# Four-layer graph network on one core: the first weights of layer 2 made inside layer 1, and every weight made one batch ahead of its product

## The chip, the cores and the metric

One core of one Trainium2 chip runs the whole program. The metric is device microseconds (us) of one execution; lower is better. Three runs of the kernel before gave 1958.09, 1960.70 and 1961.96 us, so the median is 1960.7 us.

The core has five engines that run side by side, each through its own fixed list of instructions: TensorE (PE; its weight loads are shown as PEld), VectorE (DVE), ScalarE (ACT), GpSimd (POOL) and SyncE (SP, which issues the transfers). An instruction starts when the one ahead of it on its engine is through and when the semaphores that it waits for are set. So an instruction that waits holds up everything behind it on its engine.

## The reference

There are 16 batches of 1024 nodes with 64 features, and one adjacency matrix for all. Each layer attends over neighbours, adds the result to `x` and normalises; the layers follow each other.

```python
x = _layernorm(x + _L0_gnn_ref(x, L0_gnn_W, L0_gnn_a, adj), axis=-1)
x = _layernorm(x + _L1_gnn_ref(x, L1_gnn_w0, L1_gnn_b0, L1_gnn_wa, L1_gnn_ba, adj), axis=-1)
x = _layernorm(x + _L2_gnn_ref(x, adj, L2_gnn_W, L2_gnn_a), axis=-1)
x = _layernorm(x + _L3_gnn_ref(x, adj, L3_gnn_Wh, ...), axis=-1)

def _L2_gnn_ref(input, adj, W, a):
    h = jnp.matmul(input, W)
    s1 = jnp.einsum('bnf,f->bn', h, a[:Fout, 0])
    s2 = jnp.einsum('bnf,f->bn', h, a[Fout:, 0])
    e = s1[:, :, None] + s2[:, None, :]
    e = jnp.where(e > 0, e, ALPHA * e)
    masked = jnp.where(adj[None, :, :] > 0, e, NEG_INF)
    attention = jax.nn.softmax(masked, axis=-1)
    return jax.nn.elu(jnp.matmul(attention, h))
```

## The kernel before, in words

The program is `fast_path`; a general path behind it runs only when a check at the end asks for it. P is 128, D is 64, N is 1024, C = 8 chunks of 128 nodes, B = 16 batches. `x` stays in four tiles of SBUF, one for each group of four batches.

**Layer 2** is `gat_layer(..., zero_mean=True)`. For batch b and chunk k, `unit` (L1011) is one DVE instruction (L1013) over 128x1024 elements: the larger of `G` and a factor `q`, times the adjacency `aT`. It is the masked weight `e` of chunk k, without its division. `product` (L1019) feeds it to four PE passes (L1025), which add up the batch's sum `y` over its eight chunks. What surrounds them, for a pair of batches (b, b+1 with b even):

- `prep_x` (PE transposes, ACT copies), `prep_s` (PE) and `prep_top` (DVE, then a POOL all-reduce) find the scores and their maximum.
- `prep_p`: DVE computes `down` and `up` (L958, L960), ACT computes `p` and `q` (L963, L965).
- `prep_G(b, h)` for the halves h = 0, 1: two matmuls into a PSUM tile `pg` (L978), which has one buffer in layer 2, and one ACT exponential (L987) into `G`. So the matmuls of half 1 wait for the exponential of half 0.
- `prep_v`: eight ACT scalings and a copy (L997, L999) into `vals`, the weights of the product.
- the ends of a batch: `evict` (ACT, L1044), `project` (PE, L1057), `divide` (DVE, L1100, L1102), `quotients` (eight ACT scalings L1112 and an exponential L1123), `residual` (DVE, L1128, L1129), `norm` (DVE, L1136 and, for odd b, seven small ones from L760 on), `root` and `shift` (ACT, DVE), `store` (eight ACT scalings, L780).

The order is written out by hand. `go` walks steps (t, k), t the batch and k the chunk: at each it makes `unit(k)` of batch t, lets the product of two units earlier follow (`LAG`), and then runs the tasks that the table `slots` has for (t, k). A place such as (-1, 4) in `places` means batch b's task stands at step (b-1, 4). The engines keep this order. `store` stands at (b+4, 0) for even b and at (b+3, 4) for odd b, so both fall in steps with t even; `prep_p`, `prep_G` of a pair stand at (b-1, 1), (b-1, 4) and (b-1, 6), in steps with t odd. The tile `e` has 7 buffers in layer 2.

**Layer 1** comes before it, in four groups of four batches. `product_l1` (L1898) adds up `po` for a chunk `ic` with 16 matmuls over the group's halves `hi` and `lo`; `average` (L1909) follows with two ACT instructions (L1912, L1913) and, on DVE, four of 128x256 (L1915, L1916, L1917, L1920) and four of statistics (L1922). `po` has two buffers in PSUM, and L1917 is the last reader of one. `hi` and `lo` have two buffers each. This layer is not in a hand-written order: the scheduler places its instructions and those that are put into its `ahead` lists. Eight of layer 2's first tasks (`l2_ahead[:8]`: `prep_x`, `prep_s`, `prep_top`, `prep_p` and the matmuls of `prep_G` for batches 0 and 1) go into the last group; the two exponentials into `G` and `prep_v(0)` come after it, at L2033, since their tiles are in a pool that opens there. The last group's own normalisation (`last`) is spread over layer 2's first steps: its statistics at (0, 0) and (0, 1), its ACT rows at (0, 3), (0, 7), (1, 3), (1, 7).

**Layer 3** follows. Its first preparations are placed in layer 2's steps (15, 0) to (15, 7). The ends of the last batches stand at (16, 0) to (16, 5), ahead of layer 3's first scores (PE, L1384), exponentials (ACT, L1388) and masks (DVE, L1392).

Of the kernel before, what the change touches and what calls it, by code (L numbers as in the profile page):

```python
# [8 lines left out]
F32 = mybir.dt.float32  # L9
F32R = mybir.dt.float32r  # L10
# [6 lines left out]
P = 128  # L17
# [20 lines left out]
LAG = 2  # L38
# [544 lines left out]
def fast_path(  # L583
# [25 lines left out]
    B, N, D = x.shape  # L609
# [301 lines left out]
    def gat_layer(w, name, zero_mean, own, room=None):  # L911
# [6 lines left out]
        xT, G, pgs, pq, vals, only, stats = {}, {}, {}, {}, {}, {}, {}  # L918
        if not zero_mean:
            ring = [gp.tile([P, C, 32], F32, tag=f"only{r}", name=f"only{r}", bufs=1) for r in range(4)]  # L920
            for t in ring:
# [56 lines left out]
                nc.tensor.matmul(parts[i], w1[rows, :], xT[b][h][rows, :], start=True, stop=True)  # L978

        def exps_G(b, h):  # L980
            if h == 0:
                G[b] = gp.tile([P, 2, N], F32, tag="G", name=f"G_{name}_{b}")
            cols = slice(h * HALF, (h + 1) * HALF)
            parts = pgs[b, h]
            for i, part in enumerate(parts):
                dst = G[b][:, :, cols] if len(parts) == 1 else G[b][:, i, cols]
                nc.scalar.activation(dst, part, AF.Exp, bias=pq[b][2], scale=1.0 - ALPHA)  # L987

        def prep_G(b, h):
            scores_G(b, h)  # L990
# [1 line left out]

        def prep_v(b):
            p = pq[b - b % 2][0][:, :, b % 2]
            v = gp.tile([P, C, D], F32, tag="vals", name=f"vals_{name}_{b}", bufs=3)
            for c in range(C):
                nc.scalar.activation(v[:, c, :F], xb(b)[:, c, :F], AF.Copy, scale=p[:, c : c + 1])  # L997
            if zero_mean:
                nc.scalar.copy(v[:, :, F], p)  # L999
            else:  # L1000
                only[b] = ring[b % 4]
                nc.scalar.copy(only[b][:, :, b % 2], p)
            vals[b] = v

        def attention(b):
# [3 lines left out]
            begins, closes = b % 2 == 0 or not joint, b % 2 == 1 or not joint  # L1009

            def unit(k):  # L1011
                e = gp.tile([P, N], F32, tag="e", name="e", bufs=7 if zero_mean else 10)
                nc.vector.scalar_tensor_tensor(  # L1013
                    e, G[b - b % 2][:, b % 2, :], pq[b - b % 2][1][:, k, b % 2 : b % 2 + 1], aT[:, k, :],
                    ALU.max, ALU.mult,
                )
                return e
# [164 lines left out]
        for b in range(0, B, 2):  # L1182
            halves = (range(CH), range(CH, C)) if zero_mean else (range(C), ())
            chain = [
                lambda b=b: prep_x(b, 0), lambda b=b: prep_x(b, 1), *(lambda b=b, c=c: prep_s(b, c) for c in halves),
                lambda b=b: prep_top(b), lambda b=b: prep_p(b), lambda b=b: prep_G(b, 0),
                lambda b=b: prep_G(b, 1), lambda b=b: prep_v(b), lambda b=b: prep_v(b + 1),
            ]
            if zero_mean:
                places = (-2, 0), (-2, 1), (-2, 5), (-2, 6), (-2, 7), (-1, 1), (-1, 4), (-1, 6), (-1, 2), (0, 4)  # L1190
            else:
                places = (-3, 3), (-3, 3), (-3, 7), (-3, 7), (-2, 1), (-2, 3), (-2, 7), (-1, 3), (-1, 4), (0, 4)
            if b == 0 and not zero_mean:
                chain[6:8] = [lambda f=f, h=h: f(0, h) for f in (scores_G, exps_G) for h in range(2)]
                ahead = chain[:-1]
                at(0, 4, chain[-1])
                continue
            if b == 2 and not zero_mean:
                places = (-2, 4), (-2, 5), (-2, 6), (-2, 6), (-2, 6), (-2, 7), (-1, 1), *places[7:]
            for task, (t, k) in zip(chain, places):  # L1200
                if b + t >= 0:
                    at(b + t, k, task)
                elif b:
                    at(0, 0, task)
                else:
# [555 lines left out]
    def prep_l1(g, q):  # L1761
# [36 lines left out]

        def back():
            if q == 0:  # L1800
                his[g] = l1["halves"].tile([P, C, 2, 2, P], F32R, tag="hi", name=f"hi{g}")
                los[g] = l1["halves"].tile([P, C, 2, 2, P], F32R, tag="lo", name=f"lo{g}")
            t = h["t"]
            pe = l1["psum"]("pe")
            for c in range(C):
                nc.tensor.transpose(pe[:, c, :], t[:, c, :], ident)
            hi, lo = his[g][:, :, q, 1, :], los[g][:, :, q, 1, :]
            nc.scalar.copy(hi, pe)
            nc.vector.tensor_tensor(h["f"], h["f"], pe, ALU.mult)
            nc.vector.tensor_tensor(lo, pe, hi.bitcast(F32), ALU.subtract)  # L1810
# [11 lines left out]
    with tc.tile_pool(name="ps_g", bufs=1, space=bass.MemoryType.PSUM, reuse_waits="tile") as ps_g, tc.tile_pool(  # L1822
# [64 lines left out]
    l2_ahead, l2_go = gat_layer(later["w2"], "l2", True, 6, room=dict(  # L1887
        xT=lambda: [ep.tile([P, C, D], F32, tag="v", name="xT").rearrange("p c d -> p (c d)") for _ in range(2)],
        g=lambda: l1["psum"]("pg").rearrange("p (i c) q -> p i (c q)", i=2),
    ))  # L1890
    l1_psum = ExitStack()
    ps_l = l1_psum.enter_context(tc.tile_pool(name="ps_l", bufs=2, space=bass.MemoryType.PSUM, reuse_waits="tile"))
    with tc.tile_pool(name="l1", bufs=2, reuse_waits="tile") as pool:
# [36 lines left out]
        for g in range(NG):  # L1930
            ahead = [[] for _ in range(C)]
            for q in range(2 if g + 1 < NG else 0):

                for ic, task in zip((q, q, q, q, q + 1, q + 2, q + 2, q + 4, q + 5), prep_l1(g + 1, q)):
                    ahead[ic].append(task)
            if g + 1 == NG:
                for ic, task in zip((1, 2, 3, 3, 4, 5, 6, 6), l2_ahead):
                    ahead[ic].append(task)
            st = pool.tile([P, C * GB, 6], F32, tag="st1", name=f"st{g}")
            for ic in range(C):  # L1940
                po = product_l1(g, ic)
# [15 lines left out]
    l1_pools.close()  # L1957

    l3a = ctx.enter_context(tc.tile_pool(name="l3a", bufs=2, side="right", reuse_waits="tile"))

# [212 lines left out]
```

## Time and profile before

| what | value |
|---|---|
| median of three runs | 1960.7 us |
| the profiled execution, its own time | 1960.41 us |
| its span in the trace | 1958.4 us |
| PE busy / DVE busy / ACT busy in the span | 1879.0 / 1762.2 / 1330.3 us |
| mean granted clock of PE | 0.984 |
| last `po` matmul of layer 1 | starts at 418.8 us |
| first `unit` of layer 2 | 423.62 us |
| last `unit` of layer 2 starts | 631.44 us |
| first exponential of layer 3 | 642.24 us |

The trace lists every instruction of one execution with start, duration, and what ended the idle time before it. A table by stretches gives the busy time of each engine in a stretch, and the clock that PE was granted there (1.00 is full). The chain of work that ended last gives 54% of the span to PE and 37% to DVE.

### The profile page before, as it was taken

The page shows a single profiled execution, that of the slowest core. Times are in us where ns is not written, and L with a number is a line of the kernel's source. Part 1 is how long each engine was busy: PE and PEld are TensorE (multiplying, and loading weights), DVE is VectorE, ACT ScalarE, POOL GpSimd, SP SyncE. Part 2 cuts the span into 40 slices and gives each one's busy share as a digit, 9 for nine tenths or more (in the row PEclk, how much of TensorE's full clock was granted, in tenths as well). Part 3 has the DMA queues.
Part 4 walks back from the last instruction along what each step waited for, and adds up shares of the span by engine and source line. Part 5 has one row for each costly group of instructions (what it writes and reads, how often), then busy time and mean ns, then how long its engine had stood idle before and what let it go on. Part 6 is the DMA issues. An engine that isn't in the chain of part 4 may idle for free.

```text
span 1958.4 us, 25722 instructions
## 1 busy us (share of the span) xinstructions
PE 1879.0 (96%) x9505; PEld 766.5 (39%) x9505; DVE 1762.2 (90%) x2950; ACT 1330.3 (68%) x2337; POOL 80.5 (4%) x78
## 2 busy tenths in 40 slices
PE   8999989989888999999999999999999999999985
PEld 4444347753332333333333333333333333333332
DVE  6899988879999777798999989989999899998997
ACT  4566658766776786767767767677676776776653
POOL 0000000000000000000000000000000000000001
PEclk9999989999999999999999999999999999999998
DMA  7000000000000110000000100000000100010000
GB/s 180 1 1 1 1 1 1 1 1 1 1 1 12 44 55 12 12 15 25 12 17 12 28 18 12 17 18 23 17 12 18 28 12 17 12 29 17 12 17 18
DMA packets 45746, 35.87 MB, mean 18 GB/s; under 512 B 37295, under 2 KB 37616, under 8 KB 45614
## 3 DMA queue, kind: packets, MB, share of 16 engines
q1 hardware_dynamic: 43534, 33.64, 6.7%
q8 instruction: 76, 1.25, 0.3%
q10 hardware_dynamic: 2080, 0.52, 0.1%
q14 instruction: 56, 0.46, 0.1%
HBM read 29.45 MB, written 4.70 MB: 17 GB/s over the span
## 4 chain that ended last, share of the span: by engine, by line
PE 54%; DVE 37%; ACT 6%; issue 2%; DMA 1%; POOL 0%; SPq 0%; DVEq 0%; POOLq 0%; ACTq 0%
PE y L1399 15%; PE s L1384 14%; DVE e L1392 10%; DVE e L1013 9%; PE po L1902 5%; PE y_l L1025 4%; DVE e L1557 4%; DVE junk L1549 3%; PE s L1539 3%; PE y L1564 3%; PE u_l L1037 2%; ACT e L1388 2%; ACT x L780 1%; PE ph2T L1500 1%; DVE bn L1136 1%
## 5 line engine op out<-in xcount | busy, mean ns | idle before, releaser
L1388 ACT ACTIVATE e<-s,shift 128x1024 f32<-128x1024 f32 x512 | 540.4, 1125 | 225.8 <-PE s L1384 225.8
L1392 DVE TENSOR_TENSOR e<-e,aT 128x1024 f32<-128x1024 f32 x512 | 596.6, 1216 | 13.2 <-ACT e L1388 13.0
L1384 PE MATMUL s<-hT 64*128 64x512 f32 x2048 | 492.8, 605 | 1.2 <-ACT hT L1367 0.9
L1399 PE MATMUL y<-e,vals 128*64 128x512 f32 x2048 | 485.5, 601 | 5.5 <-DVE e L1392 4.3
L1013 DVE SCALAR_TENSOR_TENSOR e<-G_l,q,aT 128x1024 f32<-128x1024 f32 x256 | 315.7, 1276 | 2.6 <-ACT G_l L987 2.4
L1384 PEld LDWEIGHTS s<-hT 64*128 64x128 f32 x2048 | 184.8, 186 | 288.7 <-issue 149.8
L1025 PE MATMUL y_l<-e,vals_l 128*64 128x512 f32 x1024 | 257.3, 621 | 27.8 <-DVE e L1013 21.0
L1399 PEld LDWEIGHTS y<-e,vals 128*64 128x64 f32 x2048 | 135.9, 137 | 273.7 <-issue 203.0
L1557 DVE TENSOR_TENSOR e<-e,aT 128x1024 f32<-128x1024 f32 x128 | 156.2, 1225 | 9.5
L1549 DVE SCALAR_TENSOR_TENSOR junk<-e,aN 128x1024 bf16<-128x1024 f32 x120 | 146.2, 1218 | 0.0
L1544 ACT ACTIVATE e<-s,shift 128x1024 f32<-128x1024 f32 x128 | 138.6, 1116 | 0.4 <-PE s L1539 0.4
L1564 PE MATMUL y<-e,h2v 128*64 128x512 f32 x512 | 127.4, 600 | 0.9 <-DVE e L1557 0.9
L1539 PE MATMUL s<-h2T 64*128 64x512 f32 x512 | 125.8, 591 | 0.0
L1025 PEld LDWEIGHTS y_l<-e,vals_l 128*64 128x64 f32 x1024 | 62.5, 139 | 160.9 <-issue 78.4
L1902 PE MATMUL po<-hi,aR 128*128 128x512 f32 x256 | 102.4, 401 | 10.0 <-ACT hi L1814 6.2
L1327 POOL PARTITION_ALL_REDUCE gtop<-top x48 | 54.3, 1130 | 1271.1 <-DVE top L1325 1016.2
L1902 PE MATMUL po<-lo,aR 128*128 128x512 f32 x256 | 100.6, 394 | 0.0
L780 ACT ACTIVATE x<-m,bn_shift,bn_rstd 128x64 f32<-128x64 f32 x256 | 89.1, 433 | 15.6 <-DVE bn_shift L771 15.5
L1539 PEld LDWEIGHTS s<-h2T 64*128 64x128 f32 x512 | 50.0, 186 | 60.1 <-issue 36.5
L1431 ACT COPY zT<-poT 64x512 f32<-64x512 f32 x124 | 72.1, 582 | 1.3 <-PE poT L1426 0.2
L1564 PEld LDWEIGHTS y<-e,h2v 128*64 128x64 f32 x512 | 36.6, 138 | 76.4 <-issue 58.5
L997 ACT ACTIVATE vals_l<-x,p 128x64 f32<-128x64 f32 (+1 forms) x256 | 64.7, 342 | 0.0
(274 smaller groups left out, 1863.9 us busy)
## 6 DMA issues: line engine op xcount, KB each, us to landing
r<-inverse SPq DMA_DIRECT2D x62, 256.0 KB
adj<-in_adj_dram SPq DMA_DIRECT2D x16, 512.0 KB
out_dram<-res SPq DMA_DIRECT2D x15, 256.0 KB
x<-in_x_dram SPq DMA_DIRECT2D x14, 256.0 KB
rows<-yT SPq DMA_DIRECT2D x62, 4.0 KB
x<-in_x_dram ACTq DMA_DIRECT2D x2, 256.0 KB
sums<-rows SPq DMA_DIRECT2D x31, 8.0 KB
inverse<-rt SPq DMA_DIRECT2D x31, 8.0 KB
```

Source lines behind the costliest of these rows:

```text
L1013: nc.vector.scalar_tensor_tensor(e, G[b - b % 2][:, b % 2, :], pq[b - b % 2][1][:, k, b % 2 : b % 2 + 1], aT[:, k, :], ALU.max, ALU.mult,)
L1025: nc.tensor.matmul(held["y"][h * D : (h + 1) * D, :], vals[b][:, k, :], e[:, h * HALF : (h + 1) * HALF], start=(k == 0), stop=(k == C - 1),)
L1384: nc.tensor.matmul(s[:, i, :], hT[rows, k * P : (k + 1) * P], hT[rows, cols], start=True, stop=True)
L1388: nc.scalar.activation(e, s, AF.Exp, bias=shifts[b, n])
L1392: nc.vector.tensor_tensor(e, e, bc_mid(aT[:, k, h * HALF : (h + 1) * HALF], 2), ALU.mult)
L1399: nc.tensor.matmul(held[h][i * D : (i + 1) * D, :], vals[b][:, k, :], e[:, i, :], start=(k == 0), stop=(k == C - 1),)
L1539: nc.tensor.matmul(s[:, i, :], hT[rows, (i + k // CH) % 2, k % CH * P : (k % CH + 1) * P], hT[rows, 0, :], start=True, stop=True,)
L1544: nc.scalar.activation(e, s, AF.Exp, bias=shifts[b])
L1549: nc.vector.scalar_tensor_tensor(junk.rearrange("p c q -> p (c q)").bitcast(BF16), e.rearrange("p i q -> p (i q)"), 1.0, aN[:, k, :], ALU. ...
L1557: nc.vector.tensor_tensor(e, e, aT[:, k, :].rearrange("p (i q) -> p i q", i=2), ALU.mult)
L1564: nc.tensor.matmul(held["o"][h * D : (h + 1) * D, :], vals["out", b][:, k, :], e[:, h, :], start=(k == 0), stop=(k == C - 1),)
L1902: nc.tensor.matmul(po.rearrange("p q k f -> p (q k f)"), aR[:, k, ic * P : (ic + 1) * P], e[:, k].rearrange("p q k f -> p (q k f)"), start ...
```

## The change

Layer 2's weights `e` no longer have seven buffers that are used in turn. They have eight fixed places, one for each chunk k: two tiles of four places, with the tags and the room of the `hi` and `lo` of layer 1's groups 0 and 2. For this, `hi` and `lo` of even groups move to a new pool `both`, with one buffer each, which stays open until layer 2 ends; those of odd groups stay in layer 1's pool, with one buffer each.

At step (t, k), `go` now first issues the product of (t, k) and then the unit of (t+1, k), into the place that this product has just read. The eight units of batch 0 are made in layer 1's last group, after the exponentials into `G` and `prep_v(0)`, which move there too, into room of layer 1 (`l1["pool"]`, tag `t`) and of the epilogue pool (`ep`, tag `m`). With the units, the preparation of later pairs moves a batch earlier: `prep_x` from (-2, 0) to (-3, 0), and so on to `prep_p` from (-1, 1) to (-2, 1) and `prep_G` from (-1, 4), (-1, 6) to (-2, 4), (-2, 6). `prep_v` and the ends of a batch keep their places. The pair of batches 2 and 3 has places of its own, from (0, 0) to (0, 5). The pools of layer 1 are closed, and one of layer 3 opened, at step (5, 0).

```diff
@@ gat_layer
         def exps_G(b, h):
+            apart = room and b == 0
             if h == 0:
-                G[b] = gp.tile([P, 2, N], F32, tag="G", name=f"G_{name}_{b}")
+                G[b] = room["G"]() if apart else gp.tile([P, 2, N], F32, tag="G", name=f"G_{name}_{b}")
             cols = slice(h * HALF, (h + 1) * HALF)
-            parts = pgs[b, h]
+            parts = [pgs[b, h][0][:, i, :] for i in range(2)] if apart else pgs[b, h]
             for i, part in enumerate(parts):
-                dst = G[b][:, :, cols] if len(parts) == 1 else G[b][:, i, cols]
+                dst = G[b][:, :, cols] if len(parts) == 1 else of_pair(b, i)[:, cols]
                 nc.scalar.activation(dst, part, AF.Exp, bias=pq[b][2], scale=1.0 - ALPHA)
+
+        def of_pair(b, i):
+            return G[b][i] if isinstance(G[b], list) else G[b][:, i, :]
...
             def unit(k):
-                e = gp.tile([P, N], F32, tag="e", name="e", bufs=7 if zero_mean else 10)
+                e = room["e"](k) if room else gp.tile([P, N], F32, tag="e", name="e", bufs=10)
                 nc.vector.scalar_tensor_tensor(
-                    e, G[b - b % 2][:, b % 2, :], pq[b - b % 2][1][:, k, b % 2 : b % 2 + 1], aT[:, k, :],
+                    e, of_pair(b - b % 2, b % 2), pq[b - b % 2][1][:, k, b % 2 : b % 2 + 1], aT[:, k, :],
                     ALU.max, ALU.mult,
                 )
...
             if zero_mean:
-                places = (-2, 0), (-2, 1), (-2, 5), (-2, 6), (-2, 7), (-1, 1), (-1, 4), (-1, 6), (-1, 2), (0, 4)
+                places = (-3, 0), (-3, 1), (-3, 5), (-3, 6), (-3, 7), (-2, 1), (-2, 4), (-2, 6), (-1, 2), (0, 4)
+                if b == 2:
+                    places = (-2, 0), (-2, 0), (-2, 1), (-2, 1), (-2, 1), (-2, 3), (-2, 4), (-2, 5), *places[8:]
...
         if room:
             ahead[-3:-1] = [lambda f=f, h=h: f(0, h) for f in (scores_G, exps_G) for h in range(2)]
+            ahead += [room["begin"], *(lambda k=k: made.update({k: work[0][0](k)}) for k in range(C))]
...
                         if t < B:
                             unit, product, _ = work[t]
-                            e = unit(k)
-                            behind(lambda product=product, k=k, e=e: product(k, e), LAG if zero_mean else 2 * LAG)
+                            if room:
+                                product(k, made.pop(k))
+                                if t + 1 < B:
+                                    made[k] = work[t + 1][0](k)
+                            else:
+                                e = unit(k)
+                                behind(lambda product=product, k=k, e=e: product(k, e), 2 * LAG)
@@ prep_l1, back
-                his[g] = l1["halves"].tile([P, C, 2, 2, P], F32R, tag="hi", name=f"hi{g}")
-                los[g] = l1["halves"].tile([P, C, 2, 2, P], F32R, tag="lo", name=f"lo{g}")
+                home = l1["halves"] if g % 2 else l1["both"]
+                his[g] = home.tile([P, C, 2, 2, P], F32R, tag="hi", name=f"hi{g}", bufs=1)
+                los[g] = home.tile([P, C, 2, 2, P], F32R, tag="lo", name=f"lo{g}", bufs=1)
@@ fast_path
+        begin=lambda: l1.update(
+            e=[l1["both"].tile([P, CH, N], F32, tag=t, name=f"e_{t}", bufs=1) for t in ("hi", "lo")]
+        ),
+        e=lambda k: l1["e"][k // CH][:, k % CH, :],
...
-                for ic, task in zip((1, 2, 3, 3, 4, 5, 6, 6), l2_ahead):
+                for ic, task in zip((0, 0, 1, 1, 1, 2, 2, 2, 3, 3, 3, 3, 3, 4, 4, 5, 5, 6, 6, 7), l2_ahead):
                     ahead[ic].append(task)
...
-    for task in l2_ahead[8:]:
-        task()
...
+        extra.setdefault((5, 0), []).append(open_l3a)
         ending = l2_go(extra)
     gat.close()
+    both.close()
```

More of the change, by code (lines that the diff above doesn't have):

```diff
@@ L917, in gat_layer @@
         F = D - 1 if zero_mean else D
-        xT, G, pgs, pq, vals, only, stats = {}, {}, {}, {}, {}, {}, {}
+        xT, G, pgs, pq, vals, only, stats, made = {}, {}, {}, {}, {}, {}, {}, {}
         if not zero_mean:
@@ L994, in prep_v @@
             p = pq[b - b % 2][0][:, :, b % 2]
-            v = gp.tile([P, C, D], F32, tag="vals", name=f"vals_{name}_{b}", bufs=3)
+            if room and b == 0:
+                v = room["vals"]()
+            else:
+                v = gp.tile([P, C, D], F32, tag="vals", name=f"vals_{name}_{b}", bufs=3)
             for c in range(C):
@@ L1221, in go @@
                             unit, product, _ = work[t]
-                            e = unit(k)
-                            behind(lambda product=product, k=k, e=e: product(k, e), LAG if zero_mean else 2 * LAG)
+                            if room:
+                                product(k, made.pop(k))
+                                if t + 1 < B:
+                                    made[k] = work[t + 1][0](k)
+                            else:
+                                e = unit(k)
+                                behind(lambda product=product, k=k, e=e: product(k, e), 2 * LAG)
                         elif t == B and k == 0:
@@ L1889, in fast_path @@
         g=lambda: l1["psum"]("pg").rearrange("p (i c) q -> p i (c q)", i=2),
-    ))
+        G=lambda: [l1["pool"].tile([P, C, P], F32, tag="t", name=f"G{i}").rearrange("p c q -> p (c q)") for i in range(2)],
+        vals=lambda: ep.tile([P, C, D], F32, tag="m", name="vals", bufs=4),
+        begin=lambda: l1.update(
+            e=[l1["both"].tile([P, CH, N], F32, tag=t, name=f"e_{t}", bufs=1) for t in ("hi", "lo")]
+        ),
+        e=lambda k: l1["e"][k // CH][:, k % CH, :],
+    ))
+    both = ExitStack()
+    l1["both"] = both.enter_context(tc.tile_pool(name="both", bufs=1, reuse_waits="tile"))
     l1_psum = ExitStack()
@@ L1956, in fast_path, with open_l3a @@
             last = [root, shift] + [lambda c=c, rows=rows: rows(c) for c in range(C * GB // 8)]
-    l1_pools.close()
-    l3a = ctx.enter_context(tc.tile_pool(name="l3a", bufs=2, side="right", reuse_waits="tile"))
+    l3a = None
+    def open_l3a():
+        nonlocal l3a
+        l1_pools.close()
+        l3a = ctx.enter_context(tc.tile_pool(name="l3a", bufs=2, side="right", reuse_waits="tile"))
     slots, mids = {}, {}
```

## The prediction

> **What bounds the kernel now.** I read the page first, then a table by stretches, then the waits of DVE, then the timelines of ACT, PE and DVE around layer 2. The page says PE, but that is an average. In layer 2 (first unit 423.62, last one ending 632.72) DVE is full and PE is not:
>
> ```profile
> PE 1879.0 (96%) x9505; PEld 766.5 (39%) x9505; DVE 1762.2 (90%) x2950; ACT 1330.3 (68%) x2337; POOL 80.5 (4%) x78
> ...
> 385.00:390.00 5.00, 5.00 (x22) 4.11 (x23) 3.17 (x17) 1.32 (x4) 0.43 (x1) 1.00 0.00 0
> ...
> 415.00:420.00 5.00, 5.00 (x26) 3.86 (x24) 2.31 (x8) 0.87 (x4) 0.00 (x0) 1.00 0.00 0
> 420.00:425.00 5.00, 0.09 (x1) 0.00 (x0) 4.64 (x17) 4.97 (x16) 0.00 (x0) 0.90 0.01 2
> ...
> 500.00:550.00 50.00, 43.51 (x216) 16.92 (x212) 49.35 (x105) 35.05 (x117) 2.47 (x2) 1.00 0.00 1
> ```
>
> The columns after a stretch's length are the busy time of PE, PEld, DVE, ACT, POOL, then the granted clock. In layer 1's last group PE is full (5.00) and DVE idles: over 385 to 420 its busy time sums to 22.64, so 12.4 of 35 us are free. Between 420 and 425 PE stands still. In 500 to 550 DVE is busy 49.35 of 50. And its waits between 425 and 633 come to 2.9 us:
>
> ```profile
> DVE e L1013 <- ACT G_l L987: 2.4, 1, 2.4
> DVE l_s L948 <- PE ps L940: 0.5, 1, 0.5
> ```
>
> So before, layer 2 is a sum of DVE instructions, with every other engine just in time. How close "just in time" is, ACT shows from `down` (DVE, 598.12) on, in step t = 13:
>
> ```profile
> 598.30 0.31 ACT L963 ACTIVATE p<-l_s,down 128x16 f32<-128x16 f32 x1 [2.04 <-DVE down L958]
> ...
> 598.72 2.01 ACT L997 ACTIVATE vals_l<-x,p 128x63 f32<-128x63 f32 x8
> ...
> 601.76 1.12 ACT L987 ACTIVATE G_l<-pg,up 128x1024 f32<-128x1024 f32 x1 [0.57 <-PE pg L978]
> 602.77 1.75 ACT L1112 ACTIVATE v<-po,rt 128x64 f32<-128x64 f32 x8
> ...
> 605.10 1.10 ACT L987 ACTIVATE G_l<-pg,up 128x1024 f32<-128x1024 f32 x1
> 606.09 2.77 ACT L780 ACTIVATE x<-m,bn_shift,bn_rstd 128x64 f32<-128x64 f32 x8
> ```
>
> The second half of `G` ends at 606.20, 8.1 us after `down`; unit (14, 0), which needs it, starts about 606.46. The stores (L780, 2.77) come right behind: ACT takes them in the even step, after the chain.
>
> **The change, part by part.** *Units in layer 1.* Eight units at 1.21 us (3.67 for three, L1013) are 9.7 us of DVE work that fits into the 12.4 free ones as a sum. By place it does not all fit: the changed order puts them between L1917 of chunk 2 and L1916 of chunk 4, some ahead of the L1917 that frees a `po` buffer. Before, L1917 ran at 401.95, 405.54, 409.12, 412.48. With three units ahead of it the third ends about 410.9, so the PE's next `po` starts at 411.0 instead of 408.1 (2.9 late), and the one after 2.4 late again: layer 1's PE work ends about 424.3 instead of 419.05. Half of the gain is given back: +5.3 against −9.7. If DVE caught up between the chunks it would be 0 to 2.9; if the units lay denser, up to 9.7.
>
> *Layer 2's start.* Units (1, 0), (1, 1) follow at 425.8 to 428.7, then the group's last average, moments and the next pair's scores. `prep_p` of batch 2 comes about 435.1. ACT then has the rows of the last group (L780 x8, 2.8) and `vals` (2.0) ahead of the first `G` half: it ends about 441.5, PE's `pg` of half 1 waits for it with products (0, 6), (0, 7) behind, and unit (1, 6) waits for (0, 6)'s place. Unit (2, 0) comes out at 446.3 to 450, I take 448.8; before it is 447.32. Steps 1 and 2 hold the ends of batch 0 alone, so unit (4, 0) is at about 473.2 against 473.88: −0.7 (bounds −3 and +2). About 4.4 us of ends are only put off: they return at the tail.
>
> *The steady state.* This is the main term. `prep_p` and `prep_G` move from odd steps to even ones, and the stores stand in even steps. So after `down` at D, ACT has, by the rows: p and q 0.60, store L780 2.67, `vals` 2.01, `G` half 0 1.12, quotients 1.75 with exponential 0.54, `G` half 1 1.10; half 0 ends at D + 6.4, half 1 at D + 9.7 (before: 4.8 and 8.1). DVE comes to the first unit that needs it after six units and 0.45 of small work, D + 7.8. PE is caught too: `pg` of half 1 (1.13) waits for half 0 in the single buffer, product (t, 7) stands behind it, and unit (t+1, 7) waits for that product because the place is now fixed. At full clock: `pg` to 7.5, product to 8.4, unit (t+1, 7) from 8.65, unit (t+2, 0) at 9.86 instead of 7.76: 2.1 us lost in each of five pairs, 10.3.
>
> Products (t, 4) to (t, 6) have their units since a batch ago and are soon done, so PE idles 4.95 us (D + 1.5 to 6.45) every second batch. The nearest row is the same length:
>
> ```profile
> 425.04 6.53 PE L1025 MATMUL y_l<-e,vals_l 128*64 128x512 f32 x16 [4.96 <-ACT bn_rstd L708]
> ```
>
> After it the clock is half:
>
> ```profile
> 424.00:425.00 1.00, 0.00 (x0) 0.00 (x0) 1.00 (x2) 0.97 (x5) 0.00 (x0) 0.52 0.00 0
> ...
> 430.00:431.00 1.00, 1.00 (x6) 0.26 (x2) 1.00 (x2) 1.00 (x5) 0.00 (x0) 0.56 0.00 0
> 431.00:432.00 1.00, 1.00 (x9) 0.50 (x5) 1.00 (x2) 1.00 (x6) 0.00 (x0) 1.00 0.00 0
> ```
>
> So for 5.9 us after resuming, four passes take 1.64 (6.53 / 4) instead of about 0.86 to 1.08, and `pg` 1.7. Unit (t+2, 0) moves to D + 11.7: 4.0 per pair, 20 in five. I take 20, since the idle of 4.95 is the row's 4.96; ends 10.3 (no throttling) and 22.5 (4.5 a pair, with `pg` at twice its time).
>
> The rule that speaks against the change stands in the Trainium skill, TensorE: Matmul & The Clock Gate, HAM oscillation: gaps of more than about 3.4 us without matmuls bring the clock down, again in every round of a loop. The same page, What's actually happening, lets the clock return after about 3.4 busy us, and here the row shows 5.9. By the page's figure a pair would lose an estimated 3.6 instead of 4.0, and the whole 2 us less.
>
> *The tail.* The last unit now ends at T = 632.72 − 0.7 + 20 = 652.0, with the last batch's products and two batches' ends behind it and no units beside them. Before, ACT after the last unit had two stores, a copy, quotients, exponential:
>
> ```profile
> 633.99 2.76 ACT L780 ACTIVATE x<-m,bn_shift,bn_rstd 128x64 f32<-128x64 f32 x8
> 636.65 0.57 ACT L1044 COPY yT_l<-y_l 128x512 f32<-128x512 f32 x1
> 637.12 2.78 ACT L780 ACTIVATE x<-m,bn_shift,bn_rstd 128x64 f32<-128x64 f32 x8
> 639.91 1.76 ACT L1112 ACTIVATE v<-po,rt 128x64 f32<-128x64 f32 x8
> ...
> 642.24 1.10 ACT L1388 ACTIVATE e<-s,shift 128x1024 f32<-128x1024 f32 x1
> ```
>
> That is 9.5 us to layer 3's first exponential. Now ACT serially has what units covered before: quotients of batch 13 (their `rt` at T − 3.7, done at T − 1.3), layer 3's copies and squares and the root of batch 13's pair, which waits for the late statistics (eight copies and squares at about 1.1 each or less; last at T + 7.1, an estimate), quotients and exponential of batch 14 (2.3), `vals` and shifts (1.6), and then the same list (8.4): T + 19.4, so +9.9. If DVE's late ends interleave better, 8; if PE at half clock holds the copies up, 12.
>
> *Hidden.* Two more, shorter exponentials for the first `G` and its `vals` move into layer 1, where ACT is busy 0.87 to 5.00 of 5; without that cover 2 us. POOL's all-reduces move a batch earlier, POOL at 4%. The first adjacency transfer of layer 3 on SP has to wait for product (15, 7), and those behind it on SP wait with it; its conversion is some 30 us later, so nothing.
>
> **Sum.** −0.7 + 20 + 9.9 = +29.2. Layer 3 is bound by PE and keeps its order, so the shift reaches the end: 1960.41 + 29.2 = 1989.6; the profiled execution lies 0.3 below the median of the runs shown, so 1989.
>
> **Rivals.** (a) The same collision, but PE keeps its clock: 10.3 for 20, so 1980. For it: the clock stays 1.00 for most of layer 2, with idle spells of 1.1 to 1.4 us; against: no spell as long as 4.95 was left at full clock. (b) It does as meant: the units hide in layer 1, no late `po`, chain and tail covered: −9.7, 1951. For it: DVE's 12.4 idle us. Against: ACT's order after `down`, which is written out and which adds a store of 2.67 to a chain that had 0.3 to spare. It decides the sign if `G` half 1 ends within D + 7.8 in the even steps. (c) Layer 1's gain and a milder collision cancel: within 3.9 us, which is the 0.2% that a measurement here can tell from no change; it needs a pair's loss of 0 to 1 and a tail that is half hidden.
>
> **Chances.** Forecast 0.65 (1983 to 1998), rival (a) 0.22 (1970 to 1982), (b) 0.07, (c) 0.03, and 0.03 for more than 1998. Low end: start −3, 10.3, tail +8 and 1 to 5 us of the store's delay found elsewhere, 1970; high end: +2, 22.5, +12, 1997, and one for rounding. Slower by over 0.2% is 0.90, faster 0.07, same 0.03.
>
> **What will show it.** In the profile of the changed kernel: DVE idle ahead of L1013, released by ACT `G_l` or PE `y_l`, once in every second batch, 2 to 4 us each, where now there is 2.4 in all; half clock in each of these places; `po` waiting for L1917 in layer 1's last group, some 5 us; the first exponential of layer 3 at about 671, and about 19 us between it and the last unit. If DVE stays at 49 of 50 in layer 2's stretches, the main term is wrong; if the clock stays at 1.00 there, rival (a) is right; if the last `po` matmul still starts at 418.8, the part on layer 1 is wrong.

## The result and the profile after

The changed kernel takes 1986.28 us (median of four runs, 1984.91 to 1989.35) where the kernel before, beside it on the same chip, takes 1959.39. The ratio is 1.0144, with a 95% interval of 1.0131 to 1.0157: it is slower by 1.4%. The profiled execution has a span of 1983.0 us against 1958.4, 24.6 more. The times below that split this difference are all from these two traces.

The page's first line, two stretches of layer 2 (busy time of PE, PEld, DVE, ACT, POOL, then the granted clock), and the largest wait of DVE between 400 and 680 in the profile of the changed kernel:

```profile
PE 1878.8 (95%) x9505; PEld 770.3 (39%) x9505; DVE 1763.0 (89%) x2950; ACT 1328.2 (67%) x2339; POOL 78.8 (4%) x78
```

```profile
500.00:550.00 50.00, 42.40 (x210) 17.53 (x208) 44.97 (x93) 28.72 (x95) 2.47 (x2) 0.97 0.00 1
550.00:600.00 50.00, 39.25 (x175) 14.51 (x171) 42.00 (x95) 32.51 (x106) 1.23 (x1) 0.90 0.00 1
```

```profile
DVE e_lo L1020 <- PE y_l L1032: 27.8, 8, 7.8
```

The work is the same, to a microsecond on PE and DVE. But DVE, busy 49.35 of 50 us in layer 2 before, is busy 44.97 and 42.00. It now waits 27.8 us for PE, one wait of 7.8 at the start of layer 2 (unit (1, 6)), two short ones, and then one of 3.5 to 4.0 in every second batch. (The unit is now L1020, the product L1032.)

| moment or stretch | before | after | difference |
|---|---|---|---|
| last `po` matmul of layer 1 starts | 418.81 | 423.19 | +4.4 |
| unit (4, 0) starts | 473.88 | 471.54 | −2.3 |
| waits at unit (t+1, 7), t = 4 to 12, five of them | 0 | 18.8 | +18.8 |
| last unit ends | 632.72 | 649.75 | +17.0 |
| from there to layer 3's first exponential | 9.52 | 18.95 | +9.4 |
| from that exponential to the end of the span | 1316.2 | 1314.3 | −1.9 |

The last three rows add up to the 24.6 us. The last unit and the first exponential behind it:

```profile
646.12 3.63 DVE L1020 SCALAR_TENSOR_TENSOR e_lo<-G_l,q,aT 128x1024 f32<-128x1024 f32 x3
668.70 5.12 ACT L1403 ACTIVATE e<-s,shift 128x1024 f32<-128x1024 f32 x5
```

One of the five collisions, seen on ACT first (start, duration, engine, line, operation):

```profile
551.24 0.31 ACT L963 ACTIVATE p<-l_s,down 128x16 f32<-128x16 f32 x1 [3.75 <-DVE down L958]
551.46 0.30 ACT L965 ACTIVATE q<-l_s,up 128x16 f32<-128x16 f32 x1
551.65 2.75 ACT L780 ACTIVATE x<-m,bn_shift,bn_rstd 128x64 f32<-128x64 f32 x8
554.30 2.00 ACT L1004 ACTIVATE vals_l<-x,p 128x63 f32<-128x63 f32 x8
...
556.29 1.11 ACT L988 ACTIVATE G_l<-pg,up 128x1024 f32<-128x1024 f32 x1
557.30 1.70 ACT L1119 ACTIVATE v<-po,rt 128x64 f32<-128x64 f32 x8
559.04 0.63 ACT L1130 ACTIVATE m<-v 128x512 f32<-128x512 f32 x1
559.57 1.10 ACT L988 ACTIVATE G_l<-pg,up 128x1024 f32<-128x1024 f32 x1
```

and then on PE and DVE in the same microseconds:

```profile
557.46 1.59 PE L978 MATMUL pg<-xT_l,l_w 64*128 64x512 f32 x4 [4.82 <-ACT G_l L988]
558.98 1.97 PE L1032 MATMUL y_l<-e_lo,vals_l 128*64 128x512 f32 x4
```

```profile
555.09 2.43 DVE L1020 SCALAR_TENSOR_TENSOR e_lo<-G_l,q,aT 128x1024 f32<-128x1024 f32 x2
561.00 1.28 DVE L1020 SCALAR_TENSOR_TENSOR e_lo<-G_l,q,aT 128x1024 f32<-128x1024 f32 x1 [3.48 <-PE y_l L1032]
```

`down` starts at 551.07. ACT stores the odd batch (L780) before it scales `vals` and makes half 0 of `G`, so PE stands for 4.82 us ahead of the matmuls of half 1; product (8, 7) is behind these, and unit (9, 7) waits 3.48 us for the place that this product reads. The trace has its own control: at t = 2 no store is due yet.

```profile
464.54 2.00 ACT L1004 ACTIVATE vals_l<-x,p 128x63 f32<-128x63 f32 x8
...
466.54 1.10 ACT L988 ACTIVATE G_l<-pg,up 128x1024 f32<-128x1024 f32 x1
```

```profile
467.69 1.13 PE L978 MATMUL pg<-xT_l,l_w 64*128 64x512 f32 x4 [1.57 <-ACT G_l L988]
468.75 1.08 PE L1032 MATMUL y_l<-e_lo,vals_l 128*64 128x512 f32 x4
```

There half 0 starts 2.6 us after `down` (463.96), not 5.2, PE stands 1.57 us, and no unit waits. The matmuls and the product take 2.14 us together there (467.69 to 469.83), and 3.49 us in the place above (557.46 to 560.95), where PE had half clock.

### The profile page after: what moved, and what is told of

The parts are those of the page before. It is cut to its first block, busy times and chain, and to the rows that moved or that the text cites. A ratio compares the mean times of both kernels' runs of the same rounds, so it can differ in the third digit from the quotient of the medians.

```text
span 1983.0 us, 25751 instructions
## 1 busy us (share of the span) xinstructions
PE 1878.8 (95%) x9505; PEld 770.3 (39%) x9505; DVE 1763.0 (89%) x2950; ACT 1328.2 (67%) x2339; POOL 78.8 (4%) x78
## 4 chain that ended last, share of the span: by engine, by line
PE 61%; DVE 28%; ACT 8%; issue 2%; DMA 1%; POOL 0%; SPq 0%; DVEq 0%; POOLq 0%; ACTq 0%
PE y L1414 17%; PE s L1399 16%; DVE e L1407 7%; PE y_l L1032 5%; PE po L1926 4%; PE s L1554 4%; PE y L1579 4%; DVE e_hi L1020 3%; DVE e L1572 3%; ACT x L780 2%; DVE e L1020 2%; DVE junk L1564 2%; DVE e_lo L1020 2%; PE u_l L1044 2%; ACT e L1403 2%
## 5 line engine op out<-in xcount | busy, mean ns | idle before, releaser
L1020 DVE SCALAR_TENSOR_TENSOR e<-G_l,q,aT 128x1024 f32<-128x1024 f32 x128 | 158.2, 1278 | 0.2
L1032 PE MATMUL y_l<-e,vals_l 128*64 128x512 f32 x512 | 122.0, 606 | 2.3 <-DVE e L1020 2.3
L780 ACT ACTIVATE x<-m,bn_shift,bn_rstd 128x64 f32<-128x64 f32 x256 | 88.4, 428 | 15.6 <-DVE bn_shift L771 15.5
L1020 DVE SCALAR_TENSOR_TENSOR e_lo<-G_l,q,aT 128x1024 f32<-128x1024 f32 x56 | 69.8, 1268 | 20.1 <-PE y_l L1032 20.0
L1020 DVE SCALAR_TENSOR_TENSOR e_hi<-G_l,q,aT 128x1024 f32<-128x1024 f32 x56 | 70.4, 1278 | 0.3 <-PE y_l L1032 0.3
L978 PE MATMUL pg<-xT_l,l_w 64*128 64x512 f32 x120 | 39.6, 741 | 32.8 <-ACT G_l L988 32.8
```

What stands on the lines that cost most here:

```text
L1020: nc.vector.scalar_tensor_tensor(e, of_pair(b - b % 2, b % 2), pq[b - b % 2][1][:, k, b % 2 : b % 2 + 1], aT[:, k, :], ALU.max, ALU.mult,)
L1032: nc.tensor.matmul(held["y"][h * D : (h + 1) * D, :], vals[b][:, k, :], e[:, h * HALF : (h + 1) * HALF], start=(k == 0), stop=(k == C - 1),)
```

## Experiments

Each is timed against the kernel before on the same chip, whose medians were 1956.7 to 1957.5 us. Differences "to the changed kernel" are against its 1986.28. It was timed on another chip, where the kernel before took 1959.39, 1.9 to 2.7 us more than here, and these differences are uncertain by as much. By the ratios to the kernel before they are 9.0 us less (e1), 6.3 less (e4), 5.5 less (e11), 2.9 less (e5) and 5.5 more (e6).

**e1: one store moved.**

```diff
             for b in range(B):
                 places = ends[b % 2]
...
+            if zero_mean and b % 2 and b < 13:
+                places = [*places[:-1], (3, 7)]
```

> Changed kernel, but the stores of the odd batches 1 to 11 stand three chunks later, at (b+3, 7), behind both halves of G in the even steps (batch 13 keeps its place). Theory (ACT's queue after down makes the units wait): without 2.67 us of store G half 0 ends 3.7 us after down and half 1 at 7.1, both ahead of the units that need them, so the five waits of 3.5 to 4.0 us at unit (t+1, 7), 18.8 us in all, shrink to under 0.5 each, the granted clock stays at 1.00 there, and the time is 1986.3 - 18 = about 1968 (1965 to 1972). Rival A (the fixed places leave no slack for the product, whatever ACT does): waits of over 2 us a pair stay, time 1978 to 1987. Rival B (the store is only late elsewhere and something else waits for it): the waits go and others of the same sum come, time within 4 of 1986.

Measured 1976.99 us, 9.3 less than the changed kernel, ratio to before 1.0098 (1.0080 to 1.0116). The waits went as the theory says: the five shrank from 18.8 to two of about 1 us (1.13 and 0.96), with the store now behind `G`. Against the expectation the clock did not stay at 1.00 everywhere. PE waits 2.16 to 2.19 us for `G` in all five places, in three of them the matmuls behind take 1.13 us and no unit waits, and in the two with a wait they take 2.07 and 1.72 us. So what is left of the waits stands where the clock was halved. One of these two:

```profile
546.97 2.07 PE L978 MATMUL pg<-xT_l,l_w 64*128 64x512 f32 x4 [2.17 <-ACT G_l L988]
```

```profile
545.81 1.10 ACT L988 ACTIVATE G_l<-pg,up 128x1024 f32<-128x1024 f32 x1
...
549.68 1.10 ACT L988 ACTIVATE G_l<-pg,up 128x1024 f32<-128x1024 f32 x1
550.68 2.75 ACT L780 ACTIVATE x<-m,bn_shift,bn_rstd 128x64 f32<-128x64 f32 x8
```

The last unit ends at 632.27 instead of 649.75. But the time came out above the range: from the last unit to the first exponential it is now 23.3 us instead of 19.0. The store of batch 11, which the edit moved too, fell into step 14 ahead of layer 3's first copies. (The trace is of the fastest of the four runs, 1972.73.) So the collision is what it was thought to be, and rival B holds for 4 us.

**e2: the preparation moved, the units not.** The kernel before with the changed kernel's table of places, and nothing else.

> Kernel before, with its seven buffers and its units in the step of their product, but the preparation of each later pair at the places of the changed kernel, a batch earlier. Theory (the collision costs only because units stand one batch ahead, in fixed places): PE still idles 3 to 5 us ahead of the matmuls of half 1 in the even steps and the clock drops there, but G is needed a batch later and the units have free buffers, so DVE waits less than 1 us a pair: 1959 +- 4. Rival (ACT's order costs by itself, through PE's idle time, the half clock and the buffers of e): 1966 or more.

Measured 1963.91 us, ratio 1.0034 (1.0024 to 1.0044), 7 us above the kernel before. As a time that lies between the two expectations; but they were written when the kernel before took 1959.39, and as a difference, 7 us are what the rival has (1966 is 6.6 more). Its reason does not hold, though. In the steady state the theory holds: from 456 to 640 DVE has no wait at all. Not even PE's idle time of 3 to 5 us is there: it waits for `G` 0.9 us at most, since its products come later. What is lost lies at the start, where batches 2 and 3 have the places meant for units a batch ahead: DVE waits 4.4, 2.1, 1.6 and 0.9 us between 427 and 452, 9.0 in all, against 2.9 in the kernel before. So ACT's order alone costs nothing later on; with seven buffers and `G` needed a batch later there is room for it.

**e3 and e11: PE kept busy while it waits.** Matmuls whose result is not read stand ahead of those of half 1: 16 from batch 4 on in e3, seven from batch 6 on in e11, whose edit this is.

```diff
+        def fill(b):
+            pf = ps_t.tile([P, HALF], F32, tag="t", name="fill")
+            for j in range(7):
+                nc.tensor.matmul(pf, w1[:D, :], xT[b][0][:D, :], start=True, stop=True)
+
         def prep_G(b, h):
+            if zero_mean and h and b > 4:
+                fill(b)
             scores_G(b, h)
```

> Changed kernel, plus 16 matmuls of 64x512 into an unused PSUM tile ahead of the matmuls of G half 1 of each pair from batch 4 on, in PE's idle time (about 3.5 us at full clock); their result is not read. Theory (PE idles 4.8 us, its clock halves, and the half clock makes 1.5 us of the 3.75 that each of five pairs loses): the clock stays 1.00 there, waits at unit (t+1, 7) fall to about 2.2 each, time 1986.3 - 7.5 = about 1979 (1976 to 1982). Rival (the clock does not matter here, the wait is ACT's alone): waits stay at 3.5 to 4.0, time 1985 to 1988.

Measured 2031.09 us, ratio 1.0371 (1.0350 to 1.0392): a mis-sized experiment. Its trace has 26 passes of one fill in 11.3 us, 0.43 us each and two for a matmul, so 16 matmuls take over 13 us, neither the 3.5 expected here nor the 9 that e11 was sized by, and each pair waited about 11 us. It says nothing of the clock. With seven:

> Changed kernel, plus 7 matmuls of 64x512 of about 0.56 us each into an unused PSUM tile ahead of the matmuls of G half 1 for batches 6 to 14 (16 of them took 9 us and were too long); their result is not read. They fill 3.9 of the 4.8 us in which PE waits. Theory (half clock makes about 1.5 of the 3.75 us that each of five pairs loses): clock 1.00 there, waits at unit (t+1, 7) about 2.2 each, time 1986.3 - 7.5 = about 1979 (1976 to 1982). Rival (the clock is no part of the wait): waits 3.5 to 4.0 as before, time 1985 to 1988.

Measured 1980.05 us, 6.2 less than the changed kernel, ratio 1.0116 (1.0100 to 1.0131). The clock stayed at 1.00 (a stretch over the third wait), and the waits are 3.24 us:

```profile
554.00:566.00 12.00, 12.00 (x54) 4.69 (x52) 8.62 (x22) 8.43 (x25) 0.00 (x0) 1.00 0.00 1
```

```profile
550.15 5.84 PE L996 MATMUL fill<-xT_l,l_w 64*128 64x512 f32 x13
555.41 0.69 PE L978 MATMUL pg<-xT_l,l_w 64*128 64x512 f32 x1
...
557.21 1.08 PE L1039 MATMUL y_l<-e_lo,vals_l 128*64 128x512 f32 x4
```

The seven were too long as well, 13 passes in 5.84 us instead of the 3.9 expected (the matmuls of `pg`, four passes in 1.13 us, were the wrong row to size them by: those are on two halves of the rows in turn). The fill ran on past the end of half 0 (554.99, when the matmuls could have begun) by about 1 us, so the wait without it would be some 2.3 us, the 2.2 of the theory; that last step is worked out, not measured. The measured part, 18.8 to 16.2 us of waits although PE did more, is enough to reject the rival. That the time falls in the expected range is in part luck: it fell by 5.5 to 6.2 us, and the waits account for 2.6.

**e4: half 1 behind the product.**

```diff
-                places = (-3, 0), (-3, 1), (-3, 5), (-3, 6), (-3, 7), (-2, 1), (-2, 4), (-2, 6), (-1, 2), (0, 4)
+                places = (-3, 0), (-3, 1), (-3, 5), (-3, 6), (-3, 7), (-2, 1), (-2, 4), (-2, 7), (-1, 2), (0, 4)
```

> Changed kernel, but G half 1 of a pair at (b-2, 7) instead of (b-2, 6), so that product (t, 7) and unit (t+1, 7) stand ahead of its matmuls. Theory (two paths lead from ACT's late half 0 to DVE: through PE's product (t, 7), and through G half 1 itself, 1.5 us shorter at half clock): the wait for PE at unit (t+1, 7) goes, and a wait for ACT G at unit (t+2, 0) of about 2 to 2.5 us takes its place; time 1986.3 - 7 = about 1979 (1976 to 1982). Rival (only PE's order is at fault, G half 1 would be in time): both waits gone, 1966 to 1972.

Measured 1979.66 us, 6.6 less, ratio 1.0112 (1.0094 to 1.0130), in the range of the theory. The wait goes one unit further, to (t+2, 0), and is 2.85, 2.46, 1.99, 2.05 and 2.84 us, 12.2 in all. The first and the third:

```profile
498.81 1.28 DVE L1020 SCALAR_TENSOR_TENSOR e_hi<-G_l,q,aT 128x1024 f32<-128x1024 f32 x1 [2.85 <-PE y_l L1032]
556.44 1.28 DVE L1020 SCALAR_TENSOR_TENSOR e_hi<-G_l,q,aT 128x1024 f32<-128x1024 f32 x1 [1.99 <-ACT G_l L988]
```

Only the third is released by `G`, as was expected of all five. The other four are released by the product (t+1, 0), which now stands behind the matmuls of half 1. Half 1 is late by itself there, too: in the first place its exponential ends at 497.95, 2.0 us after the unit ahead has ended (495.96). So more than one path leads from ACT's late half 0 to DVE, and cutting the longest one leaves the next.

**e5: the start of layer 2.**

```diff
+                if b == 0:
+                    places = *places[:9], (0, 6)
...
-        for p, task in zip(((0, 0), (0, 1), (0, 3), (0, 7), (1, 3), (1, 7)), last):
+        for p, task in zip(((0, 0), (0, 1), (0, 6), (0, 7), (1, 3), (1, 7)), last):
```

> Changed kernel, but in step 0 ACT's first two row groups of layer 1's last normalisation, at (0, 3) before, and vals of batch 1, at (0, 4) before, stand at (0, 6), behind both halves of G for batches 2 and 3. Theory (the 7.83 us wait at unit (1, 6) is ACT's queue after the first down: rows 2.74 and vals 2.2 ahead of G half 0): G half 0 starts right after q, PE's gap of 7.1 us ahead of the second half's matmuls falls to about 1, the wait to 1 to 2, unit (2, 0) comes 6 us earlier, time 1986.3 - 6 = about 1980 (1977 to 1983). Rival (unit (2, 0) is held by the late scores of batch 2, or the rows are only late elsewhere): 1984 to 1988.

Measured 1981.45 us, 4.8 less, ratio 1.0129 (1.0114 to 1.0144). The wait at unit (1, 6) fell from 7.83 to 3.17 us, not to 1 to 2, and 1.3 us came back in short waits behind it; the last unit ends 2.9 us earlier (646.81), not 6. So ACT's queue is a cause of this wait, and gave about half of what was expected.

**e6: layer 3's preparation a step earlier.**

```diff
-        places = [(15, j) for j in (0, 1, 2, 3, 4, 5, 6, 7)]
+        places = [(14, j) for j in (0, 1, 2, 3, 4, 5, 6, 7)]
```

> Changed kernel, but the eight tasks of layer 3's first preparation stand in step 14 instead of 15. Theory (the 19 us between the last unit and layer 3's first exponential are ACT's work in a row, 6 of it those tasks, which units no longer cover): the stretch shrinks by 5 to 6 us, time 1986.3 - 5.5 = about 1981 (1978 to 1983). Rival (the stretch is set by batches 14 and 15 themselves, products, project, quotients, and the tasks lie beside it): the stretch stays within 1.5 us, time 1984 to 1988.

Measured 1989.89 us, 3.6 more, ratio 1.0172 (1.0158 to 1.0187): neither. The stretch did shrink, 18.95 to 15.7 us, but the last unit ended 5.8 us later (655.52), since in step 14 PE waits for ACT's copies with the products behind it:

```profile
PE phT L1373 <- ACT xT L1360: 5.4, 1, 5.4
PE pn L1336 <- ACT hsq L1388: 3.4, 1, 3.4
```

**e7 and e8: everything together.** e7 has e5, e6, the stores of the odd batches 1 to 9 at (b+3, 7), and the stores of batches 12 and 13 behind layer 3's first exponentials. e8 adds an order by hand for DVE in layer 1's last group.

> Changed kernel with the three edits together: stores of batches 1, 3, 5, 7, 9 at (b+3, 7); rows and vals of batch 1 behind G in step 0; layer 3's first preparation in step 14. Besides, the stores of batches 12 and 13 go behind layer 3's first exponentials (they stood ahead of the scores). Theory (what the change costs is three collisions in ACT's queue, and the gain in layer 1 is real): last unit ends at 632.3 - 6 = about 626, first exponential of layer 3 about 11 to 13 us later, at 638 against 642.2 in the kernel before; time 4 us below the kernel before, 1950 to 1957. Rival (the change costs more than ACT's queue: fixed places, room, the ring of one): waits appear in other places, time 1960 or more.

> As e7_three, and in layer 1's last group DVE keeps the order as written, each average ahead of the units that follow it (two units after chunks 2 to 4, one after 5 and 6). Theory (units ahead of L1917 held a po buffer 2.1 us and cost PE 3.4 us of clock besides): PE's wait for L1917 goes below 1 us, layer 1's last matmul starts about 420 instead of 423.2, time 2 to 3 us below e7_three. Rival (the delay only moves to the start of layer 2, which waits for the same units): within 1 us of e7_three.

Measured 1970.45 us (ratio 1.0067, 1.0055 to 1.0079) and 1973.17 us (1.0079, 1.0066 to 1.0092). Both missed. e7 carries e6's loss: the last unit ends at 635.92, not 626. Besides, the way from the first exponential to the end is 1319.9 us in both, against 1314.3 in the changed kernel; no run shows why. In e8 PE still waited 2.2 us for a `po` buffer, so the order did not do what it was for, and nothing follows from it but that this order is no better.

**e9: without the collisions, and e10: one part of it in the kernel before.** e9 is e7 without e6, with these stores last of all; e10 is the kernel before with only the second branch.

```diff
+            if zero_mean and b in (1, 3, 5, 7, 9):
+                places = [*places[:-1], (3, 7)]
+            elif zero_mean and b in (12, 13):
+                places = [*places[:-1], (18 - b, b - 6)]
```

> Changed kernel without the collisions found so far: stores of batches 1, 3, 5, 7, 9 at (b+3, 7), rows and vals of batch 1 behind G in step 0, layer 3's first preparation left in step 15, and the stores of batches 12 and 13 as the last of the ends that run in layer 3's first bursts. Theory (step 15 has no units any more, so the 9.7 us that left layer 2 come back as an uncovered tail, and without waits the change is worth about nothing): last unit ends at 649.8 - 18.8 - 3 = about 628, first exponential of layer 3 some 13.5 us later, at 642, as in the kernel before; time within 3 of the kernel before. Rival (the waits were all that it cost): first exponential at 637 or earlier, time 5 us or more below the kernel before.

> Kernel before, with one edit: the stores of batches 12 and 13, which stand ahead of layer 3's first scores, run as the last of the ends in layer 3's first bursts. Theory (5.5 us of ACT in a row between last unit and first exponential are these stores, and nothing there needs them): first exponential at about 638 to 639 instead of 642.2, time 3 us below the kernel before (1 to 5). Rival (layer 3's first bursts are short of ACT time and give it back, as in e7, where the way from the first exponential to the end was 4 us longer): within 1.5 of the kernel before.

e9 takes 1960.96 us, ratio 1.0019 (1.0010 to 1.0028): 3.7 us above the kernel before, 0.7 outside the expected bound; the first exponential is at 644.81, and the rival's gain of 5 us is not there. e10 takes 1953.54 us, ratio 0.9978 (0.9969 to 0.9987), and is faster than both kernels: 3.7 us below the kernel before, where 1 to 5 were expected. The two have the same stores out of the way, and so show the change with most of its collisions gone. The ends of their tails, ACT of e9 and then of e10:

```profile
639.97 0.30 ACT L1353 ACTIVATE shift<-gtop,headroom 128x1 f32<-128x1 f32 x1 [0.27 <-POOL gtop L1348]
640.17 0.57 ACT L1051 COPY yT_l<-y_l 128x512 f32<-128x512 f32 x1
642.49 1.74 ACT L1119 ACTIVATE v<-po,rt 128x64 f32<-128x64 f32 x8 [1.75 <-DVE rt L1109]
644.27 0.63 ACT L1130 ACTIVATE m<-v 128x512 f32<-128x512 f32 x1
644.81 5.12 ACT L1409 ACTIVATE e<-s,shift 128x1024 f32<-128x1024 f32 x5
```

```profile
632.56 0.29 ACT L1334 ACTIVATE shift<-gtop,headroom 128x1 f32<-128x1 f32 x1 [0.39 <-POOL gtop L1329]
632.81 0.59 ACT L1044 COPY yT_l<-y_l 128x512 f32<-128x512 f32 x1
635.15 1.75 ACT L1112 ACTIVATE v<-po,rt 128x64 f32<-128x64 f32 x8 [1.75 <-DVE rt L1102]
636.93 0.63 ACT L1123 ACTIVATE m<-v 128x512 f32<-128x512 f32 x1
637.47 5.12 ACT L1390 ACTIVATE e<-s,shift 128x1024 f32<-128x1024 f32 x5
```

From `shift` on the two are alike. But the last unit ended at 629.45 in e9 and at 631.63 in e10, so the whole tail is 15.4 us against 5.8. The difference, 9.5 us, is about what eight units take (9.7 by the price of the prediction). That the last unit ends only 2.2 us earlier in e9, with eight units fewer ahead of it, is in part layer 1, whose last `po` matmul starts at 423.32 against 417.71, and in part the 8.4 us that DVE still waits for PE in layer 2, against 3.0 us of waits in e10. Step 15 of the changed order has no units, and its products, layer 3's first preparation and the ends of batches 14 and 15 lie bare.

**e12: half a step.** e9 with layer 3's preparation from (14, 4) to (15, 3), and the store of batch 11 at (14, 1).

> As e9_without_collisions, with layer 3's first preparation four chunks earlier, from (14, 4) to (15, 3), and the store of batch 11 at (14, 1), so that ACT is free for it. Theory (the tail of e9, 15.4 us from last unit to first exponential, is the chain of that preparation and batch 15's products, one behind the other, since units no longer cover the first): about 4 us of the chain move beside step 14's units, first exponential 3 to 5 us earlier than in e9 (644.8), time 3 to 5 us below e9, 1956 to 1958. Rival (as in e6, PE waits for the preparation in step 14 and holds up units by as much): within 2 of e9, 1959 to 1963.

Measured 1962.84 us, ratio 1.0024 (1.0014 to 1.0035): within 2 of e9, the rival's side. Tail 13.5 us, last unit 632.25: what the tail lost, the units gained. The edit has a flaw of its own, though: the store of batch 11 stood right behind that of batch 10 and held `yT` up, and PE was idle for 7.8 us ahead of `project`.

## Why the prediction came out as it did

**Forecast and rivals.** Forecast 1989 us, slower; measured 1986.28. (Its last step takes 0.3 us off where the reason given would add them: 1990.) The clock halved in each of the five places, so rival (a) is out; the units found their place in layer 1 but ACT's queue after `down` was late, so (b) and (c) are out.

**Units in layer 1.** Two late `po` starts were forecast, 2.9 and 2.4 us. There was one:

```profile
410.52 0.47 PE L1926 MATMUL po<-hi,aR 128*128 128x512 f32 x1 [2.14 <-DVE t L1941]
```

Layer 1's last matmul came 4.4 us later and not 5.3. That the size is near is luck, since the split is another: 2.14 of waiting, and in the stretch 410 to 415 a clock of 0.66, which takes 5 x 0.34 = 1.7 us of full speed away and was not in the sum. The other 0.6 are not accounted for. The size itself is uncertain by about 1 us: that matmul starts at 417.56 and 417.71 in e2 and e10, which have the layer 1 of the kernel before, and between 421.6 and 424.9 in the experiments with that of the changed one.

**Layer 2's start.** Unit (4, 0) at 473.2 forecast, 471.54 measured: −2.3 instead of −0.7, inside the bounds. The wait at unit (1, 6), for which no length was given, was 7.83, and by e5 the cause named is behind at least 4.7 of it:

```profile
444.47 2.67 DVE L1020 SCALAR_TENSOR_TENSOR e_lo<-G,q,aT 128x1024 f32<-128x1024 f32 x2 [7.83 <-PE y_l L1032]
```

**The steady state.** 4.0 us for each pair were forecast, 20 in all (3.6 by the prediction's estimate from the page of the Trainium skill named below); the waits are 3.59, 3.77, 3.48, 3.96 and 3.97, together 18.8. (The forecast's own prices at half clock, 1.7 us for `pg` and 1.64 for the product, add up to 3.5 a pair and 17.5 in all; 4.0 needs `pg` at twice its 1.13.) The trace splits the waits: from the first matmul of half 1 to the end of product (t, 7) PE takes 2.14 us at full clock (t = 2), and 3.60, 3.79, 3.49, 3.97 and 3.99 us in the five places. So the clock's share is 8.1 us, where 9.7 were forecast (20 less 10.3), and what ACT's lateness costs at full clock is the other 10.6, where 10.3 were. Of the runs, e1 shows ACT's queue as the cause, e4 the path over PE's product (and in one place of five that over `G`), and e11 that the clock has a share, of which it measured 0.5 us a pair. The term that was mis-sized is the length of half clock. The two stretches of the third wait, and one over the fourth:

```profile
557.00:560.00 3.00, 2.54 (x8) 0.71 (x10) 0.52 (x1) 2.97 (x11) 0.00 (x0) 0.67 0.00 0
560.00:563.00 3.00, 3.00 (x14) 0.98 (x12) 2.00 (x2) 0.94 (x2) 0.00 (x0) 0.77 0.00 0
...
584.00:598.00 14.00, 10.44 (x42) 3.93 (x44) 9.93 (x21) 10.42 (x34) 0.00 (x0) 0.76 0.00 0
```

At half clock for a time h, a stretch of length s has a mean of 1 − h/(2s). So h is 2 x (3 x 0.33 + 3 x 0.23) = 3.4 us for the third wait and 2 x 14 x 0.24 = 6.7 for the fourth; the first two are like the third, the last like the fourth. The forecast's 5.9, taken from one row, counts from the moment PE resumes. In the fourth and fifth place the clock was halved already at 585.3 and 616.0, while PE stood still, and PE resumed at 587.56 and 618.21. After resuming, half clock lasted 3.1, 3.4, 3.4, 4.6 and 4.6 us, less than 5.9 everywhere. This cost the forecast little: where half clock covered the matmuls and the product whole, in the last two places, the wait is the 4.0 of the forecast, and where it did not, it is 3.48 to 3.77. The page of the Trainium skill that the forecast weighed against its row (TensorE: Matmul & The Clock Gate, What's actually happening) gives about 3.4: three of five agree with it, and two lie between it and the 5.9.

**The tail.** +9.9 forecast, +9.4 measured, 18.95 us in place of 19.4, and the same instructions in the same order on ACT. What the prediction did not see is what it means. It booked the tail as a price of its own, next to a gain of 9.7 in layer 1. e9 and e10 speak for their being one thing, by the size of the two (9.5 against 9.7): work that moves out of a DVE-bound stage into the stage ahead saved nothing here, since the last step was left with its other work uncovered.

**Layer 3.** The shift was to reach the end whole; 1.9 us of it were made up after the first exponential. That is no more than traces differ by: this way takes 1312.8 to 1316.2 us in all of them but e7 and e8.

**Open.** Whether some order lets the changed kernel's last step overlap with units was not settled: e6 and e12 moved layer 3's preparation and lost in step 14 what they won in step 15. Nor was an order tried with success that keeps the units of layer 1 from holding a `po` buffer.

## What to carry to other kernels

Making work one step ahead of its use shifts everything that feeds it, too: look at each queue that the moved preparation passes, in the step where it lands, and at what else stands there. Work moved out of a full engine pays only if the stage can end earlier by it, so follow the last step first and ask what covers its serial chain. And before moving work at all, look for instructions in that chain that nobody waits for: two stores put behind the next stage's first exponentials (e10) brought 0.2% that the large change did not.

## What was not expected of the hardware

The clock of PE was halved after shorter idle times than the 4.96 us of the row that the prediction used: after 2.14 us in layer 1 (clock 0.66 in 410 to 415), and in e1, where PE waited 2.17 us for `G`, the matmuls of half 1 took 2.07 us instead of 1.13. The rule of the Trainium skill that the prediction weighed (TensorE: Matmul & The Clock Gate, HAM oscillation), gaps of more than about 3.4 us, gives no warning of these two places.

The length of the gap alone does not decide, though. In e1 the same wait, 2.16 to 2.19 us, left the clock whole in three places of five, and in e4 a longer one did:

```profile
553.19 1.13 PE L978 MATMUL pg<-xT_l,l_w 64*128 64x512 f32 x4 [3.30 <-ACT G_l L988]
```

In the trace of the changed kernel the five half clocks begin at 496.6, 527.3, 558.0, 585.3 and 616.0 us. These are 30.7, 30.7, 27.3 and 30.7 apart, which is 9, 9, 8 and 9 times 3.41, and each lasts once or twice 3.41 us. So the clock seems to change on a fixed beat of 3.41 us. The short gaps that halved it lie within one beat: in layer 1, half clock begins at 411.2, and the beat ahead of it, 407.8 to 411.2, holds the whole gap (408.4 to 410.5). The gap of 3.30 us in e4 (549.9 to 553.2) is parted by a beat at 551.9, by the half clocks of its own trace. No run moved a gap against the beat on purpose, so this is a reading and not a test. It does not cover everything: in the kernel before, PE had half clock from 486 to 488 us, though it had been busy without a gap since 477.7.
